# Storing the output of a residual matmul two tiles at a time, with semaphores of its own

## The chip, the core and the metric

The kernel runs on one NeuronCore of one Trainium2 chip. The metric is the device time of one execution in microseconds (us), the median of several runs. A profiled execution leaves a trace of every instruction and of every DMA packet. Engines are named as in the profile: PE (TensorE, the matmuls), PEld (its weight loads), DVE (VectorE), ACT (ScalarE), POOL (GpSimd) and SP (SyncE). ACT and SP issue DMAs here, each to a queue of its own; the transfers of both queues run on the same 16 DMA engines. "ACTq" and "SPq" in the profile are the issues of the two queues.

## What is computed

For each of 128 batch entries b, one of 8 weight matrices is picked by an index, and the product is added to the input:

```python
x = ...                      # (B=128, C=128, T=1024) float32
subjects = ...               # (128,) int32, 0..7
weights = ...                # (8, C=128, D=128) float32
w = weights[subjects]
out = x + jnp.einsum('bct,bcd->bdt', x, w)
```

Input and output are 67.1 MB each, the weights 0.5 MB, all in float32.

## The kernel before

**Tiles and slots.** A tile is four batch entries (G = 2 entries in each of H = 2 halves), 2.10 MB, and there are NT = 32 of them. SBUF holds SLOTS = 12 tiles in one tensor, x_all; tile i lives in slot i % 12. A tile's input is loaded into its slot, the sum is written over it in place, and the output is stored from there. So a slot is free for the load of tile i + 12 only when the store of tile i has landed.

**Loads.** ACT issues four loads of 512 KB for each tile (lines 203 to 207), in the order of the tiles. From tile 12 on it first waits until the slot's store has landed (line 205). Since ACT issues in order, a wait holds back every load behind it. POOL turns a landed tile into "ready" counts for PE (lines 209 to 214).

**Compute.** For each half of a tile, DVE copies the picked weights into a small tile (`place`), PE runs 8 matmuls into PSUM (`multiply`) and DVE adds the PSUM result to the slot (`add`), which raises s_added by one. So s_added counts two for each finished tile. PE starts on a tile when its four loads have landed.

**Stores.** SP issues the stores (lines 216 to 220). Tiles 0 to 19 are stored one by one; from tile 20 on two neighbours go in one store of 4.19 MB. A store of n tiles from tile i waits until s_added shows i + n + BEHIND finished tiles, with BEHIND = 4, and without BEHIND from tile 24 on (LAST = 8). A single store 0 thus waits for 5 finished tiles, store 1 for 6. The pair 20 waits for 26, the pair 22 for 28, the pair 24 (behind 22 in SP's order) for 26, the pair 26 for 28, and 28 for 30. The last pair, 30, is issued outside the loop (line 240) when all 32 are finished.

**Semaphores.** A slot has one semaphore, s_slot, for its loads and its store: each landed load and each landed store adds 16 to it. `emptied(i)` (line 123) computes the count at which the slot is free for tile i. In the last part each pair's store raises the even slot's semaphore alone. At the end ACT waits for the stores of the last 12 tiles.

**Queue order.** No order is worked out by a scheduler around the change: loads, readiness and stores stand in the program as the loops write them, on ACT, POOL and SP.

Of the kernel before, what the change touches and what calls it, by code (L numbers as in the profile page):

```python
# [30 lines left out]
G = 2  # L31
H = 2
# [3 lines left out]
SLOTS = 12  # L36

P_SLOTS = 2

BEHIND = 4  # L40
LAST = 8

PAIR = 2

DMA = 16

# [8 lines left out]
def transfer(nc, engine, out, in_):  # L55

    later, nc._always_lower_symbolic_ap = nc._always_lower_symbolic_ap, False
    ins, outs = engine.lower_ap_dma(in_), engine.lower_ap_dma(out)  # L60
    nc._always_lower_symbolic_ap = later
    return engine.add_instruction(
        mybir.InstDMACopy(
            name=nc.get_next_instruction_name(),
            engine=engine.engine,
            ins=ins,
            outs=outs,
            mode="Copy",
            cce_op=ALU.bypass,
            queue=QUEUES[engine.engine],  # L70
        )
    )


@with_exitstack
def kernel(
    ctx: ExitStack,
    tc: tile.TileContext,
    x: bass.AP,
    subjects: bass.AP,  # L80
    weights: bass.AP,
    out: bass.AP,
):
    nc = tc.nc
    B, C, T = x.shape
    S, _, D = weights.shape
    NT = B // (G * H)

    def sbuf(name, *shape, dtype=F32):
        return ctx.enter_context(nc.sbuf_tensor(name, list(shape), dtype)).ap()  # L90


    room = -(nc.sbuf_base + -nc.sbuf_base % 32) % ALIGN
    if room:
        sbuf("room", C, room // 4)
    x_all = sbuf("x_all", C, SLOTS * H * G * T)
    xs = [
        x_all[:, i * H * G * T : (i + 1) * H * G * T].rearrange("c (q t) -> c q t", t=T)
        for i in range(SLOTS)
    ]  # L100
    w_all = sbuf("w_all", C, S, D)
    ws = [sbuf(f"w{i}", C, 1, D) for i in range(H * G)]
    zeros = sbuf("zeros", C, N)
    given, near, wrap = (sbuf(name, 1, B, dtype=I32) for name in ("given", "near", "wrap"))
    index = sbuf("index", 1, B + H * G, dtype=I32)
    ps = [
        ctx.enter_context(nc.psum_tensor(f"ps{i}", [D, G, T], F32)).ap() for i in range(P_SLOTS)
    ]

    s_given = tc.alloc_semaphore("s_given")  # L110
    s_wall = tc.alloc_semaphore("s_wall")
    s_index = tc.alloc_semaphore("s_index")
    s_zeros = tc.alloc_semaphore("s_zeros")
    s_product = tc.alloc_semaphore("s_product")
    s_added = tc.alloc_semaphore("s_added")

    s_ready = tc.alloc_semaphore("s_ready")
    s_go = tc.alloc_semaphore("s_go")

    s_slot = [tc.alloc_semaphore(f"s_slot{k}") for k in range(SLOTS)]  # L120
    s_head = tc.alloc_semaphore("s_head")

    def emptied(i):
        turns = i // SLOTS
        return DMA * (H * G + 1) * turns - (DMA * G if i >= SLOTS and i % SLOTS == 0 else 0)

    def load(engine, i, q):
        transfer(
            nc,
            engine,  # L130
            xs[i % SLOTS][:, q, :],
            x[i * H * G + q].rearrange("(a r) t -> a (r t)", r=ROWS),
        ).then_inc(s_head if i * H * G + q < G else s_slot[i % SLOTS], DMA)

    def store(i, n):
        at = i % SLOTS * H * G * T
        return transfer(
            nc,
            nc.sync,
            out[i * H * G : (i + n) * H * G].rearrange("g d t -> d g t"),  # L140
            x_all[:, at : at + n * H * G * T].rearrange("d (o t) -> d o t", o=n),
        )

    def subjects_of(i):
        _, subject = nc.values_load_multi_w_load_instructions(
            index[0:1, i] if isinstance(i, slice) else index[0:1, bass.ds(i * (H * G), H * G)],
            engines=[mybir.EngineType.DVE],
            min_val=0,
            max_val=S - 1,
            skip_runtime_bounds_check_because="the index is clamped on the chip above",  # L150
        )
        return subject

    def place(h, subject):
        for q in range(h * G, (h + 1) * G):
            copy = nc.vector.tensor_copy(ws[q], w_all[:, bass.ds(subject[q], 1), :])  # L156
        copy.then_inc(s_go, 1)

    def multiply(slot, h):
        nc.tensor.wait_ge(s_go, 1).then_inc(s_go, -1)  # L160
        nc.tensor.wait_ge(s_ready, 1).then_inc(s_ready, -1)  # L161
        for q in range(h * G, (h + 1) * G):
            for t in range(0, T, N):
                at = slot * (H * G * T) + (q * T + t)
                mm = nc.tensor.matmul(  # L165
                    ps[h][:, q % G, t : t + N],
                    ws[q][:, 0, :],
                    x_all[:, bass.ds(at, N)],
                    start=True,
                    stop=True,  # L170
                )
        mm.then_inc(s_product, 1)

    def add(slot, h):
        mine = x_all[:, bass.ds(slot * (H * G * T) + h * G * T, G * T)]
        nc.vector.wait_ge(s_product, 1).then_inc(s_product, -1)  # L176
        nc.vector.tensor_tensor(  # L177
            mine, ps[h].rearrange("d g t -> d (g t)"), mine, ALU.add
        ).then_inc(s_added, 1)

    with tc.tile_critical():  # L181

        nc.sync.dma_start(given, subjects.rearrange("(o b) -> o b", o=1)).then_inc(s_given, DMA)
        nc.sync.dma_start(w_all, weights.rearrange("s c d -> c s d")).then_inc(s_wall, DMA)

        nc.vector.memset(zeros, 0.0).then_inc(s_zeros, 1)  # L186
        nc.tensor.wait_ge(s_zeros, 1)
        for _ in range(IDLE):
            nc.tensor.matmul(  # L189
                ps[P_SLOTS - 1][:, G - 1, :N], zeros[:, :D], zeros, start=True, stop=True  # L190
            )

        nc.vector.memset(index[:, B:], 0).then_inc(s_index, 1)  # L196
        nc.vector.wait_ge(s_given, DMA)
        nc.vector.tensor_scalar(near, given, -S, S - 1, ALU.max, ALU.min).then_inc(s_index, 1)  # L198
        nc.vector.wait_ge(s_index, 2)
        nc.vector.tensor_scalar(wrap, near, 0, S, ALU.is_lt, ALU.mult).then_inc(s_index, 1)  # L200
        nc.vector.wait_ge(s_index, 3)
        nc.vector.tensor_tensor(index[:, :B], near, wrap, ALU.add).then_inc(s_index, 1)  # L202
        for i in range(NT):
            if i >= SLOTS:
                nc.scalar.wait_ge(s_slot[i % SLOTS], emptied(i))
            for q in range(H * G):
                load(nc.scalar, i, q)

        for i in range(NT):
            if i == 0:  # L210
                nc.gpsimd.wait_ge(s_head, DMA * G).then_inc(s_ready, 1)
                nc.gpsimd.wait_ge(s_slot[0], DMA * G).then_inc(s_ready, 1)
            else:
                nc.gpsimd.wait_ge(s_slot[i % SLOTS], emptied(i) + DMA * H * G).then_inc(s_ready, H)

        for i in [*range(NT - SLOTS), *range(NT - SLOTS, NT, PAIR)]:
            n = 1 if i < NT - SLOTS else PAIR
            nc.sync.wait_ge(s_added, (i + n + (BEHIND if i < NT - LAST else 0)) * H)
            if i + n < NT:
                store(i, n).then_inc(s_slot[i % SLOTS], DMA)  # L220


        nc.vector.wait_ge(s_index, 4)
        nc.vector.wait_ge(s_wall, DMA)
        subject = subjects_of(slice(0, H * G))
        for h in range(H):
            place(h, subject)
        with nc.vector.Fori(0, NT) as turn:  # L228
            subject = subjects_of(turn + 1)
            for h in range(H):  # L230
                add(turn % SLOTS, h)
                place(h, subject)
        with nc.tensor.Fori(0, NT) as turn:
            for h in range(H):
                multiply(turn % SLOTS, h)

    with tc.tile_critical() as waits:
        for i in range(NT - SLOTS, NT - PAIR, PAIR):
            nc.scalar.wait_ge(s_slot[i % SLOTS], emptied(i + SLOTS))
    last = store(NT - PAIR, PAIR)  # L240

    tc.add_manual_dep(
        last.ins,
        waits.name,
        mybir.DependencyInfo(mybir.DependencyClass.NoSync, mybir.DependencyReason.SCHED_ONLY),
        reason="the end of the program waits for it",
    )
# [27 lines left out]
```

## Time and profile before

| What | Value |
|---|---|
| Runs of the kernel | 323.47 us median of 3 (323.29 to 323.54) |
| The profiled execution | 323.24 us |
| Its span in the trace | 321.5 us |
| HBM read and written | 67.63 MB and 67.11 MB, 419 GB/s over the span |
| PE busy | 249.8 us (78%) |
| DVE busy | 165.7 us (52%) |
| Mean granted PE clock | 0.905 |
| Loads of x | 128 of 512 KB, median 34.9 us from issue to landing |
| Single stores | 20 of 2048 KB, median 15.6 us from issue to landing |
| Paired stores | 6 of 4096 KB, median 28.6 us from issue to landing |
| Matmuls | 512, mean 635 ns |
| Adds | 64, mean 2291 ns |

The page shows the span in 40 slices of 8.04 us. Its row "DMA" gives the mean busy share of the 16 DMA engines in each slice as a digit of tenths, and the row "GB/s" what they moved. In the part on DMA queues, q10 carries the loads of x (ACT's queue) and q1 the stores, the weights and the index (SP's queue); the columns are packets, MB, and the time of the packets as a share of 16 engines' span.

The trace can also be asked for single transfers. Such an answer has two lines that matter: the issues (line, queue, operation, tensors, number; the shortest, middle and longest issue in ns; first and last start in us from the start of the span), and below it the shortest, middle and longest time from an issue to the landing of its data. A timeline line gives start, length, engine, line, operation and tensors, and in brackets the idle time of the engine before it.

### The profile page before, as it was taken

Reading aid. Unit: us, or ns where it says so; the run is one execution under the profiler, and the core shown is the slowest. Engines: PE = TensorE matmul, PEld = TensorE weight load, DVE = VectorE, ACT = ScalarE, POOL = GpSimd, SP = SyncE. Lnnn points to the kernel's source line nnn. Section 1 sums busy time; section 2 is a strip of 40 time slices with the busy share of each in tenths; the row PEclk is TensorE's granted clock in tenths of the full one; section 3 lists DMA queues with packets and bytes.
Section 4 is the critical chain, followed back from the end, with each engine's and each line's share of the span. In section 5 each row is a group of like instructions: output and inputs, shape, how many; then the busy total and the mean of one; then the engine's idle time right before and its main releaser. Section 6 shows DMA issues by size and latency. Waiting matters only on the chain. (4 is left out here: it accounts for less than half of the span.)

```text
span 321.5 us, 2368 instructions
## 1 busy us (share of the span) xinstructions
PE 249.8 (78%) x518; PEld 102.8 (32%) x518; DVE 165.7 (52%) x202; POOL 0.2 (0%) x4
## 2 busy tenths in 40 slices
PE   6999999999979666866888469999769995885000
PEld 2444444444433322322333124433323332331000
DVE  2377667767773366146365361776445766066000
POOL 0000000000000000000000000000000000000000
PEclk9999999999997799779999896999978999599555
DMA  7999999999999999999999999999999999999997
GB/s 283 428 424 424 426 424 391 428 426 426 428 432 428 423 430 424 426 424 424 426 426 428 430 430 426 426 426 428 424 424 424 420 426 430 426 428 424 430 424 318
DMA packets 11700, 134.76 MB, mean 419 GB/s; under 512 B 2482, under 2 KB 3507, under 8 KB 3507
## 3 DMA queue, kind: packets, MB, share of 16 engines
q10 hardware_dynamic: 6144, 67.12, 49.7%
q1 hardware_dynamic: 5554, 67.64, 49.7%
q14 instruction: 2, 0.01, 0.0%
HBM read 67.63 MB, written 67.11 MB: 419 GB/s over the span
## 5 line engine op out<-in xcount | busy, mean ns | idle before, releaser
L165 PE MATMUL ps<-x_all,w 128*128 x512 | 244.4, 635 | 42.2 <-PEq L161 27.6
L177 DVE TENSOR_TENSOR x_all<-ps,x_all 128x2048 f32 x64 | 146.6, 2291 | 124.9 <-DVEq L176 124.9
L165 PEld LDWEIGHTS ps<-x_all,w 128*128 128x128 f32 x512 | 101.0, 203 | 186.3 <-issue 185.8
L156 DVE COPY w<-w_all 128x128 f32 x132 | 23.1, 218 | 4.1 <-DMA w_all<-in_L_cond_weights_dram 4.1
L189 PE MATMUL ps<-zeros 128*128 128x512 f32 x6 | 5.5, 1088 | 1.7 <-DVE zeros L186 1.7
L189 PEld LDWEIGHTS ps<-zeros 128*128 128x128 f32 x6 | 1.8, 328 | 3.7 <-issue 2.1
L186 DVE MEMSET zeros<- 128x512 f32 x1 | 0.5, 485 | 1.0 <-SPq L181 1.0
L198 DVE TENSOR_SCALAR near<-given 1x128 int32<-1x128 int32 x1 | 0.2, 214 | 0.7 <-DMA given<-in_itok_B_dram 0.7
L202 DVE CUSTOM_DVE_ANT_0 index<-near,wrap 1x256 uint16<-1x256 uint16 x1 | 0.3, 280 | 0.0
L200 DVE TENSOR_SCALAR wrap<-near 1x128 int32<-1x128 int32 x1 | 0.2, 216 | 0.0
L262 POOL MEMSET const-bfloat16-1.0<- 128x1 bf16 x1 | 0.1, 101 | 0.0
L262 POOL MEMSET const-uint8-127<- 128x1 uint8 x1 | 0.1, 101 | 0.0
L262 POOL MEMSET const-float32-0.0<- 128x1 f32 x1 | 0.1, 98 | 0.2 <-issue 0.2
L262 POOL MEMSET const-float32-1.0<- 128x1 f32 x1 | 0.1, 98 | 0.0
L262 DVE BASE_LOAD x1 | 0.0, 21 | 0.1
L196 DVE MEMSET index<- 1x4 int32 x1 | 0.1, 62 | 0.0
## 6 DMA issues: line engine op xcount, KB each, us to landing
x_all<-in_x_dram ACTq DMA_DIRECT2D x128, 512.0 KB, 34.9
out_dram<-x_all SPq DMA_DIRECT2D x20, 2048.0 KB, 15.6
out_dram<-x_all SPq DMA_DIRECT2D x6, 4096.0 KB, 28.6
w_all<-in_L_cond_weights_dram SPq DMA_DIRECT2D x1, 512.0 KB, 5.0
given<-in_itok_B_dram SPq DMA_DIRECT2D x1, 0.5 KB
```

Of the source, the lines that this page charges most:

```text
L156: copy = nc.vector.tensor_copy(ws[q], w_all[:, bass.ds(subject[q], 1), :])
L165: mm = nc.tensor.matmul(ps[h][:, q % G, t : t + N], ws[q][:, 0, :], x_all[:, bass.ds(at, N)], start=True, stop=True,)
L177: nc.vector.tensor_tensor(mine, ps[h].rearrange("d g t -> d (g t)"), mine, ALU.add).then_inc(s_added, 1)
L186: nc.vector.memset(zeros, 0.0).then_inc(s_zeros, 1)
L189: nc.tensor.matmul(ps[P_SLOTS - 1][:, G - 1, :N], zeros[:, :D], zeros, start=True, stop=True)
L196: nc.vector.memset(index[:, B:], 0).then_inc(s_index, 1)
L198: nc.vector.tensor_scalar(near, given, -S, S - 1, ALU.max, ALU.min).then_inc(s_index, 1)
L200: nc.vector.tensor_scalar(wrap, near, 0, S, ALU.is_lt, ALU.mult).then_inc(s_index, 1)
L202: nc.vector.tensor_tensor(index[:, :B], near, wrap, ALU.add).then_inc(s_index, 1)
L262: nc = _bacc.Bacc("TRN2", target_bir_lowering=False, num_devices=1)
```

## The change

All stores become pairs. Each pair of slots has a semaphore for its store, s_store, and s_slot counts loads alone. SP's loop runs over even tiles and waits for i + 2 + BEHIND finished tiles with BEHIND = 3 (LAST stays 8), so that the pair 0 waits for 5, the pair 2 for 7, up to 25 for the pair 20 and 27 for 22; 24, 26 and 28 wait for 26, 28 and 30 as before. ACT waits before every second tile for the landing of the pair that used its two slots, and then issues eight loads. The number of stores goes from 26 to 16, ACT's waits in the load loop from 20 to 10. Tiles, loads, matmuls, adds and the last pair's place are as they were.

```diff
-BEHIND = 4
+PAIR = 2
+
+BEHIND = 3
 LAST = 8
-
-PAIR = 2
...
-    def emptied(i):
-        turns = i // SLOTS
-        return DMA * (H * G + 1) * turns - (DMA * G if i >= SLOTS and i % SLOTS == 0 else 0)
+    s_store = [tc.alloc_semaphore(f"s_store{k}") for k in range(SLOTS // PAIR)]
+
+    def stored(i):
+        return s_store[i % SLOTS // PAIR], DMA * (i // SLOTS + 1)
+
+    def loaded(i):
+        return s_slot[i % SLOTS], DMA * H * G * (i // SLOTS + 1) - (DMA * G if i % SLOTS == 0 else 0)
...
-    def store(i, n):
+    def store(i):
         at = i % SLOTS * H * G * T
         return transfer(
             nc,
             nc.sync,
-            out[i * H * G : (i + n) * H * G].rearrange("g d t -> d g t"),
-            x_all[:, at : at + n * H * G * T].rearrange("d (o t) -> d o t", o=n),
+            out[i * H * G : (i + PAIR) * H * G].rearrange("g d t -> d g t"),
+            x_all[:, at : at + PAIR * H * G * T].rearrange("d (o t) -> d o t", o=PAIR),
         )
...
         for i in range(NT):
-            if i >= SLOTS:
-                nc.scalar.wait_ge(s_slot[i % SLOTS], emptied(i))
+            if i >= SLOTS and i % PAIR == 0:
+                nc.scalar.wait_ge(*stored(i - SLOTS))
             for q in range(H * G):
                 load(nc.scalar, i, q)
...
-                nc.gpsimd.wait_ge(s_slot[0], DMA * G).then_inc(s_ready, 1)
+                nc.gpsimd.wait_ge(*loaded(0)).then_inc(s_ready, 1)
             else:
-                nc.gpsimd.wait_ge(s_slot[i % SLOTS], emptied(i) + DMA * H * G).then_inc(s_ready, H)
-
-        for i in [*range(NT - SLOTS), *range(NT - SLOTS, NT, PAIR)]:
-            n = 1 if i < NT - SLOTS else PAIR
-            nc.sync.wait_ge(s_added, (i + n + (BEHIND if i < NT - LAST else 0)) * H)
-            if i + n < NT:
-                store(i, n).then_inc(s_slot[i % SLOTS], DMA)
+                nc.gpsimd.wait_ge(*loaded(i)).then_inc(s_ready, H)
+
+        for i in range(0, NT, PAIR):
+            nc.sync.wait_ge(s_added, (i + PAIR + (BEHIND if i < NT - LAST else 0)) * H)
+            if i + PAIR < NT:
+                store(i).then_inc(stored(i)[0], DMA)
...
         for i in range(NT - SLOTS, NT - PAIR, PAIR):
-            nc.scalar.wait_ge(s_slot[i % SLOTS], emptied(i + SLOTS))
-    last = store(NT - PAIR, PAIR)
+            nc.scalar.wait_ge(*stored(i))
+    last = store(NT - PAIR)
```

## The prediction

> **What bounds the kernel now.** First I read the DMA rows of the page.
>
> ```profile
> DMA  7999999999999999999999999999999999999997
> GB/s 283 428 424 424 426 424 391 428 426 426 428 432 428 423 430 424 426 424 424 426 426 428 430 430 426 426 426 428 424 424 424 420 426 430 426 428 424 430 424 318
> q10 hardware_dynamic: 6144, 67.12, 49.7%
> q1 hardware_dynamic: 5554, 67.64, 49.7%
> ```
>
> From the second slice to the last but one the 16 engines never rest: loads alone (slices 2 to 5), both together, and stores alone (the last four whole slices) all move about 427 GB/s. The two queues share 99.4% of the span. A tile of 2.10 MB therefore costs 2.097 / 0.427 = 4.91 us of DMA, and the time is the sum of the bytes. No edit can make it much shorter; it gets longer if both queues are ever empty together. So I look for that place. While loads run there is none: the middle load takes 34.9 us from issue to landing, and 4.91/0.4 = 12 us of that would be one tile, so about three tiles stand queued. The end is another matter. Queue waits of SP, then the last tile's loads, matmuls, adds and store:
>
> ```profile
> SPq L271 <- DMA out_dram<-x_all: 23.1, 1, 23.1
> ...
> L62 ACTq DMA_DIRECT2D x_all<-in_x_dram x2: 2260/2576/2891, 240.8 to 243.1; - x2
> DMA to landing us min/median/max: 42.2/42.6/43.0
> ...
> 274.85 10.14 PE L165 MATMUL ps<-x_all,w 128*128 x16 [5.21 <-PEq L161]
> 286.53 7.13 PE L165 MATMUL ps<-x_all,w 128*128 x16 [1.54 <-PEq L161]
> 293.90 2.29 DVE L177 TENSOR_TENSOR x_all<-ps,x_all 128x2048 f32 x1 [0.81 <-DVEq L176]
> ...
> L62 SPq DMA_DIRECT2D out_dram<-x_all x1: 601/601/601, 296.8 to 296.8; - x1
> DMA to landing us min/median/max: 23.7/23.7/23.7
> ```
>
> The last load lands at 243.1 + 43.0 = 286.1, the last add ends at 293.90 + 2.29 = 296.2, the last store is issued 0.6 later and lands at 320.5. It holds 4.19 MB, 9.8 us of DMA, so of its 23.7 us some 9 to 10 were spent behind older stores. **Those 9 us are the slack**: the last add may come that much later for nothing, and after that each us is a us of the run.
>
> **The rates that decide the end.** Four stores, two single and two paired, and two pairs of loads:
>
> ```profile
> L62 SPq DMA_DIRECT2D out_dram<-x_all x1: 663/663/663, 46.4 to 46.4; - x1
> DMA to landing us min/median/max: 13.6/13.6/13.6
> ...
> L62 SPq DMA_DIRECT2D out_dram<-x_all x1: 544/544/544, 53.5 to 53.5; - x1
> DMA to landing us min/median/max: 15.1/15.1/15.1
> ...
> L62 SPq DMA_DIRECT2D out_dram<-x_all x1: 612/612/612, 237.1 to 237.1; - x1
> DMA to landing us min/median/max: 21.9/21.9/21.9
> ...
> L62 SPq DMA_DIRECT2D out_dram<-x_all x1: 607/607/607, 257.0 to 257.0; - x1
> DMA to landing us min/median/max: 21.5/21.5/21.5
> ```
>
> ```profile
> L62 ACTq DMA_DIRECT2D x_all<-in_x_dram x2: 882/970/1059, 207.5 to 208.6; - x2
> DMA to landing us min/median/max: 34.9/35.9/36.9
> ...
> L62 ACTq DMA_DIRECT2D x_all<-in_x_dram x2: 2281/2584/2888, 214.4 to 217.3; - x2
> DMA to landing us min/median/max: 37.2/37.3/37.3
> ```
>
> The singles land at 60.0 and 68.6: 8.6 us a tile while loads run beside them, a share of 4.91/8.6 = 0.57. The first had an empty queue, so 13.6 - 8.6 = 5.0 us of it is start and finish. The page's last slice holds 8.04 x 318/427 = 6.0 us of traffic, which ends at 319.4 against the landing at 320.5; so 1.1 us is the finish and 3.9 the start. The pairs then drain in 16.9 and 16.5 us, mean 16.7: a share of 9.82/16.7 = 0.588. The loads beside the first pair land at 245.5 and 254.6, three loads on: 12.1 us a tile, share 0.40, which would give the pair 0.60. I take 0.588 (a whole pair, with its edges), so a load tile beside pairs takes 4.91/0.412 = 11.9 us, and keep 0.57 and 0.605 as ends. From a tile's landing to its last add I count 10.0 us for the last tile (286.1 to 296.2) and 13.0 for the one before (last load issued at 237.6, 36.9 to landing, add done at 287.5), whose 16 matmuls took 10.14 us at a lower clock. I take 11.5, or 10 where TensorE had waited under 2 us.
>
> **The change part by part.** *Fewer, larger stores*: 26 become 16, on SP. Ten issues of 0.54 us go from a queue that waits most of the time: nothing. Ten times 16 semaphore writes go from the engines; the page counts 2482 packets under 512 B. Bounds: nothing, and the step from 427 to 428 GB/s that the slices allow between mixed traffic and large stores alone, 0.2% of the 230 us that change, 0.5 us. I take 0.1, nearer to nothing, since slices with loads of 512 KB alone move the same as those with 4 MB stores.
>
> The Trainium skill, page "SBUF — State Buffer", section "The DMA setup-cost knee", gives each DMA a fixed 2 us and advises the largest transfers; ten fewer would by that be worth 20 us (an estimate from the page). The slices disagree: 512 KB loads alone run at 424 to 428 GB/s, so the cost overlaps here.
>
> *One wait of ACT for two slots* (L205): the even slot's loads are issued one single store later, 8.6 us. Behind that wait only loads stand. They join a queue with some 35 us to landing, which hides it; were that queue empty, each would be late in full. *POOL's waits* keep their number and meaning: nothing. *Own semaphores*: no instruction more on the path.
>
> *BEHIND 3 on pairs* (L218): pair i waits for i+5 added tiles, as single i did; the odd tile goes one add earlier. The pairs 20 and 22 wait for 25 and 27 where they waited for 26 and 28, and 24 follows 22 at once. So the store queue is ahead, and the loads, which get only 0.41 beside it, come in later; the bytes are the same. Ledger, with pair, issue, data from and to:
> - 0 at 46.4, 50.3 to 67.8 (0.7 for the slow slice 7: 8.04 x 35/426); 2, 4, 6, 8 follow without a gap to 84.5, 101.2, 117.9, 134.6, as loads come every 11.9 us.
> - 10 at 133.5 (tile 14 landed at 122.0, plus 11.5), 137.4 to 154.1. Loads had 2.8 us alone, in which they go 2.4 times as fast.
> - 12 at 152.5, 156.4 to 173.1; 14 at 172.4, 176.3 to 193.0; 16 at 192.5, 196.4 to 213.1; 18 at 212.2, 216.1 to 232.8; 20 at 231.2, 235.1 to 251.8; 22 at 250.8, 254.7 to 271.4. Gaps of 2.3 to 3.4 us.
> - 24 to 288.1; tile 24 lands at 220.3, then 11.9 us each less what the gaps give, tile 31 at 296.3; 26 to 301.1, alone from 296; 28 to 310.9.
> - Last add 296.3 + 11.5 = 307.8; issue 308.4; data from 312.3.
>
> The engines are empty from 310.9 to 312.3: **1.4 us**. The same ledger for the kernel before, at the singles' share, ends its loads at 285.4 where the trace has 286.1. Sum on the profiled execution's 323.24 (span 321.5, 1.7 around it): 323.24 - 0.1 + 1.4 = 324.5. The runs' median lies 0.23 above that execution, so 324.7; I write 324.6.
>
> Ends: with the lag between 10 and 13 and the share between 0.57 and 0.605, the last add falls between 303 and 310, the hole between nothing and 3.9 us. It is near the edge because a later add shifts the gaps too.
>
> **Rivals.**
> - *The slack suffices* (no slower). The last add stays before about 306, because the gaps in the store queue fall long and let the loads through. For it: half of the ledgers within the ends; 7 of the 9 us of slack must be used up before anything shows. Against: the odd stores go earlier in every round. Time: 323.47 - 0.1, about 323.4.
> - *The larger store gains*. Each transfer costs something that the overlap does not hide; 0.5 us at most by the slices, with the slack left: 322.8. Against: loads alone show no such cost. The skill's knee, above, is the rule for this one.
> - *The store queue takes two thirds.* If an engine's turn grew with the store, 16 pieces against 8, loads would take 14.7 us a tile, and the ledger's last add comes at 310 to 315: a hole of 3 to 8 us, 329. Against: the pairs of the trace show 0.60 at most. The Trainium skill, "DMA: Bandwidth & Descriptors", section "Queues, rings and completion order", has each engine change queues after a whole packet; that no row shows what a packet is here leaves this open.
> - *The change is not what it says*: no; the program has 16 stores of 128x8x1024 and no single one.
>
> **How the numbers follow.** Hole of 0.7 to 4 us 0.48, slack suffices 0.42, larger store gains 0.05, two thirds 0.05. A measurement of this kernel can tell about 0.2%, 0.65 us, from no change. Faster 0.05, same 0.42, slower 0.53. The predicted time is the first case's, 324.6; its own range is 324.1 to 327.0. The range for all goes from 323.0, the slack case with its gain, to 327.0, the hole of 3.9 less the gain; the two-thirds case and the gain case are left out.
>
> **What would show it.** Right: the last load lands at 293 to 298 and the last store at 306 to 311, with some 14 us to landing instead of 23.7, and the GB/s row dips in its last two slices. If that store still takes 17 us or more, the slack held. Loads of a tile landing under 11.5 us apart, or long stretches without stores, would make the share wrong; a dip anywhere earlier would mean that I missed an empty queue.

## The result, and the profile after

The changed kernel takes 324.37 us (median of 16 runs, 323.32 to 326.12) against 323.35 us (16 runs, 322.98 to 323.87) of the kernel before: ratio 1.0035, 95% interval 1.002 to 1.005. It is slower by about 1.0 us. Three of its runs lie at 325.7 us or more and thirteen at 324.7 or less, so it also scatters over 2.8 us where the kernel before scatters over 0.9. The profiled execution is one of the three: 325.97 us, span 324.2.

The page of the changed kernel, rows on DMA:

```profile
DMA  7999999999999999999999999999999999999967
GB/s 281 427 423 427 435 423 396 425 423 431 427 431 425 424 427 429 423 425 421 431 427 421 429 423 427 431 421 427 427 427 427 427 425 431 427 425 429 427 287 323
...
q10 hardware_dynamic: 6144, 67.12, 49.4%
q1 hardware_dynamic: 5394, 67.63, 49.2%
```

The last slice but one moves 287 GB/s where it moved 424 before; (427 - 287)/427 x 8.1 us = 2.7 us of traffic are missing there. The end of this execution, by the loads of the last tile, the matmuls of the last two tiles, the last add and the last store:

```profile
L62 ACTq DMA_DIRECT2D x_all<-in_x_dram x3: 2276/2888/2908, 245.5 to 251.3; - x3
DMA to landing us min/median/max: 46.1/46.2/46.6
...
286.68 8.82 PE L169 MATMUL ps<-x_all,w 128*128 x16 [2.11 <-PEq L165]
298.33 10.16 PE L169 MATMUL ps<-x_all,w 128*128 x16 [2.83 <-DVE w L160]
...
308.74 2.29 DVE L181 TENSOR_TENSOR x_all<-ps,x_all 128x2048 f32 x1 [0.81 <-DVEq L180]
...
L62 SPq DMA_DIRECT2D out_dram<-x_all x1: 600/600/600, 311.6 to 311.6; - x1
DMA to landing us min/median/max: 11.6/11.6/11.6
...
310.00:313.00 3.00, 0.00 (x0) 0.00 (x0) 1.30 (x3) 0.00 (x0) 0.72 0.20 87
```

The last line is a stretch of the window view; its last three columns are the granted clock, the share of the DMA engines and GB/s. The last load lands at 297.9 (before: 286.1), the last tile's matmuls take 10.16 us at a lower clock (granted 0.50 from 298.3 to 304.5, against 7.13 us at 1.00 for the last tile before), the last add ends at 311.0, and the engines stand four fifths idle from 310 to 313. Such a stretch, in which both queues are empty, is called a hole below. The last store then lands 11.6 us after its issue: it found nothing ahead of it.

A second trace of the same kernel (323.94 us, span 322.2) looks different at the same place:

```profile
294.61 8.82 PE L169 MATMUL ps<-x_all,w 128*128 x16 [4.58 <-PEq L165]
...
303.68 2.29 DVE L181 TENSOR_TENSOR x_all<-ps,x_all 128x2048 f32 x1 [0.81 <-DVEq L180]
...
L62 SPq DMA_DIRECT2D out_dram<-x_all x1: 601/601/601, 306.6 to 306.6; - x1
DMA to landing us min/median/max: 14.6/14.6/14.6
...
310.00:313.00 3.00, 0.00 (x0) 0.00 (x0) 0.00 (x0) 0.00 (x0) 0.50 0.99 421
```

The last add ends at 306.0, 5 us earlier, and no engine rests: 0.99 busy, 421 GB/s. The store still stands some 3 us behind older ones (14.6 against 11.6). Yet its span is 0.7 us longer than the kernel before's. A third trace (324.01 us) has the same end. So a hole explains the one of the three longest runs that was traced, and something else is needed for the rest. The two later traces are of runs somewhat below the median of 324.37; a run at the median was not traced.

### The profile page after: what moved, and what is told of

It is laid out like the page before. It is cut to its first block, busy times and chain, and to the rows that moved or that the text cites. A ratio compares the mean times of both kernels' runs of the same rounds, so it can differ in the third digit from the quotient of the medians.

```text
span 324.2 us, 2358 instructions
## 1 busy us (share of the span) xinstructions
PE 258.4 (80%) x518; PEld 105.8 (33%) x518; DVE 165.7 (51%) x202; POOL 0.2 (0%) x4
## 5 line engine op out<-in xcount | busy, mean ns | idle before, releaser
L169 PE MATMUL ps<-x_all,w 128*128 x512 | 252.9, 653 | 48.5 <-PEq L165 45.6
L169 PEld LDWEIGHTS ps<-x_all,w 128*128 128x128 f32 x512 | 104.0, 209 | 198.1 <-issue 197.6
```

The source lines that it names most:

```text
L169: mm = nc.tensor.matmul(ps[h][:, q % G, t : t + N], ws[q][:, 0, :], x_all[:, bass.ds(at, N)], start=True, stop=True,)
```

## The experiments

Each kernel was timed beside the kernel before on the same chip, and each ratio is to that. Three chips were used: one for experiments 1 to 4, one for 5, 9, 10 and 11, one for 6, 7, 8 and 12; the kernel before took 323.30, 323.19 and 323.29 us on them. Theory T, or H, is the prediction's: the hole before the last pair. Theory R, later S, is that the 4 MB stores cost something of their own.

**1. Pairs held for one tile more** (`BEHIND = 3` becomes `4` in the changed kernel).

> The changed kernel with BEHIND = 4: pairs wait for one more tile. Theory T (each store goes out at an earlier tile count, so the loads end late and the last pair finds empty queues): last load lands at 285 to 292, last add at 296 to 304, no hole; 323.3 us, ratio to before 0.999 to 1.001. Rival P (pairing itself, by its larger share and by freeing two slots at once): the last load still lands after 294 and a hole of 1 us or more stays, ratio 1.002 to 1.005. Rival R (4 MB stores slow the engines all along): ratio 1.002 or more with the last store's landing over 17 us after its issue.

Measured: 324.32 us, ratio 1.0032 (1.0022 to 1.0042). The last load lands at 286.8 and the last store of its trace is:

```profile
L62 SPq DMA_DIRECT2D out_dram<-x_all x1: 602/602/602, 297.4 to 297.4; - x1
DMA to landing us min/median/max: 23.7/23.7/23.7
```

The loads end as early as before the change and the store has its old 23.7 us, so there is no hole. And the time is still that of the changed kernel. T is right on the loads and wrong on the time; what fits is R: a loss with no hole possible, since the last store still stood 12 us behind older ones (23.7 against the 11.6 of a store with nothing ahead).

**2. Singles released one tile earlier** (`BEHIND = 4` becomes `3` in the kernel before).

> The kernel before with BEHIND = 3: single stores as before, each one tile earlier; the pairs from tile 20 on wait as in the changed kernel. Theory T: last load lands at 290 to 297, last add at 301 to 308, the slack shrinks from 9 us to 0 to 6 us and in some runs is gone; ratio 1.000 to 1.003. Rival P: the last load lands before 289 and the last store still takes over 20 us to land; ratio 0.999 to 1.001.

Measured: 323.49 us, ratio 1.0003 (0.9994 to 1.0012). In its trace:

```profile
L62 SPq DMA_DIRECT2D out_dram<-x_all x1: 600/600/600, 303.1 to 303.1; - x1
DMA to landing us min/median/max: 17.5/17.5/17.5
```

The last store is issued 6.3 us later than in the kernel before. The earlier release alone eats most of the slack, as T said, without pairs, and while slack is left it costs nothing.

**3. The last pair stored as two singles.**

```diff
-        for i in range(0, NT, PAIR):
+        for i in range(0, NT - PAIR, PAIR):
...
+        nc.sync.wait_ge(s_added, (NT - 1) * H)
+        store(NT - PAIR, 1).then_inc(stored(NT - PAIR)[0], DMA)
+        nc.sync.wait_ge(s_added, NT * H)
...
-    last = store(NT - PAIR)
+    last = store(NT - 1, 1)
```

> The changed kernel with the last pair stored as two singles, the first as soon as tile 30 is finished. Theory T: nothing moves ahead of it; tile 30's store (4.9 us) fills the wait for tile 31, so a hole of up to 4 us goes; 323.3 us, ratio 0.999 to 1.001, the last store lands 7 us or more after its issue, and the last load still lands at 293 to 298. Rival R: ratio stays 1.002 to 1.005.

Measured: 324.05 us, ratio 1.0021 (1.0012 to 1.0031), highest run 325.04. Its trace has no hole, and its last add ends early, at 303.7, so that it would have had none with a pair either. None of the 11 runs reaches the 325.7 of the changed kernel's three longest, which with 11 runs can be chance. The greater part of the loss stays with the place of the hole filled: against T as the cause of the median.

**4. Pairs released two tiles earlier** (`BEHIND = 1`).

> The changed kernel with BEHIND = 1: pairs wait for two tiles fewer, the suspected cause doubled and more. Theory T: last load lands at 301 to 306, last add near 314, a hole of 4 to 10 us; 327 to 333 us, ratio 1.013 to 1.03. Rivals P and R: stores earlier than this cost nothing new, ratio 1.002 to 1.006.

Measured: 331.38 us, ratio 1.0237 (1.0218 to 1.0255). Window view of its end:

```profile
303.00:310.00 7.00, 7.00 (x18) 2.89 (x16) 5.12 (x6) 0.00 (x0) 1.00 1.00 424
310.00:318.00 8.00, 4.00 (x10) 1.51 (x8) 5.12 (x6) 0.00 (x0) 0.89 0.01 4
318.00:328.00 10.00, 0.00 (x0) 0.00 (x0) 0.00 (x0) 0.00 (x0) 0.50 0.98 419
```

While PE and DVE finish the last tile, all DMA engines rest for 8 us, as much as the whole loss (8.1 us). The last add ends at 316.5, later still than expected. The mechanism of the hole is shown; experiments 1 and 3 show that it is not what the median run pays.

**5. Two stores of 2 MB for each pair, waits unchanged.**

```diff
-        return s_store[i % SLOTS // PAIR], DMA * (i // SLOTS + 1)
+        return s_store[i % SLOTS // PAIR], DMA * PAIR * (i // SLOTS + 1)
...
-                store(i).then_inc(stored(i)[0], DMA)
+                for j in range(i, i + PAIR):
+                    store(j, 1).then_inc(stored(i)[0], DMA)
```

> The changed kernel, waits and tile counts as they are, but each pair but the last is stored by two DMAs of 2 MB issued one behind the other, on the pair's semaphore. Theory H (the median's 1 us is the hole before the last pair): the loads end as late as in the changed kernel, ratio 1.002 to 1.004. Theory S (the 4 MB store itself slows some of the 16 engines, hole or not): ratio 0.999 to 1.001 where there is no hole.

Measured: 323.50 us, ratio 1.0003 (0.9993 to 1.0014). Two DMAs of 2 MB in place of one of 4 MB take away nearly all of the loss. But this trace's last load lands at 287.9, not as late as H assumed, so the hole went as well, and this run alone does not decide. Experiment 6 has no hole on either side.

**6. The same with BEHIND = 4**, to be set beside experiment 1.

> The kernel with pairs and BEHIND = 4, each pair but the last stored by two DMAs of 2 MB: no hole with either size of store. Theory S (one 4 MB store makes some of the 16 engines late): ratio 0.999 to 1.001, against 1.0032 with the 4 MB stores; the last part of the last store lands 0.4 to 0.6 us after the mean of its 16 parts. Rival U (two slots freed at once, or the semaphores): ratio 1.002 to 1.004, the last part 0.9 us or more behind the mean.

Measured: 323.30 us, ratio 1.0001 (0.9990 to 1.0011), against 1.0032 (1.0022 to 1.0042) with 4 MB stores. The last store of its trace:

```profile
L62 SPq DMA_DIRECT2D out_dram<-x_all x1: 612/612/612, 298.8 to 298.8; - x1
DMA to landing us min/median/max: 22.0/22.0/22.0
```

The intervals are apart, the waits, the slots and the number of semaphores are the same, and neither trace has a hole (22.0 and 23.7 us to landing): **storing each pair in one DMA of 4 MB, and not in two of 2 MB, costs about 1 us**. The expectation on the parts of the last store failed, though: its last part lands 1.05 us behind the mean of the 16, not 0.4 to 0.6.

**7 and 8. Where the 4 MB stores cost.** In the changed kernel, 4 MB stores for tiles 0 to 11 alone, or for the pairs after tile 12 alone; the other pairs but the last are two stores of 2 MB. The core of the second (the first has the opposite condition):

```diff
+    def pieces(i):
+        return PAIR if i < SLOTS else 1
...
+                for j in range(i, i + PAIR, PAIR // pieces(i)):
+                    store(j, PAIR // pieces(i)).then_inc(stored(i)[0], DMA)
```

> The changed kernel with 4 MB stores for tiles 0 to 11 alone, where the next store is always queued behind; the later pairs but the last are two DMAs of 2 MB each. Theory S1 (an engine falls behind where a 4 MB store ends with no other queued): as two_singles, ratio 0.999 to 1.001. Theory S2 (every 4 MB store makes engines late): ratio 1.001 to 1.002.

> The changed kernel with two DMAs of 2 MB for each pair of tiles 0 to 11 and one store of 4 MB for each later pair, most of which end with no other queued. Theory S1: as the changed kernel, ratio 1.002 to 1.004, the last part of the last store 0.9 us or more behind the mean of the 16 unless a hole came before it. Theory S2: ratio 1.001 to 1.002.

Measured: first 323.50 us, ratio 1.0007 (0.9998 to 1.0016); after 323.87 us, ratio 1.0023 (1.0013 to 1.0032). The cost is seen with the later stores, as S1 said, but this does not show S1. The two intervals overlap a little, and the later stores are 9 of the 15 pairs that were varied: the loss of 1.0035 shared equally among the 15 would give 1.0014 and 1.0021, inside both intervals.

**9. Pairs held for two tiles more** (`BEHIND = 5`).

> The changed kernel with BEHIND = 5, one more step away from any hole: last load at 278 to 286, last store 20 us or more to landing. Theory H: ratio 0.999 to 1.001. Theory S: ratio 1.002 to 1.004, as with BEHIND = 4.

Measured: 327.10 us, ratio 1.0124 (1.0106 to 1.0143). Neither theory had this. The GB/s row of its page, and two stretches:

```profile
GB/s 275 432 420 426 430 424 432 420 422 246 426 424 426 434 426 421 426 424 434 424 422 428 430 428 424 424 424 436 424 422 424 424 430 430 424 424 424 436 428 307
```

```profile
66.00:73.00 7.00, 7.00 (x17) 2.91 (x16) 5.07 (x7) 0.00 (x0) 1.00 0.97 414
73.00:77.00 4.00, 4.00 (x11) 1.84 (x10) 2.87 (x4) 0.00 (x0) 1.00 0.50 107
```

The hole is at the front. The first pair now goes out when 7 tiles are finished (60.6 us) and lands at 74; the twelve slots' loads are all in by 64, and nothing may be loaded or stored until the pair has landed. So for pairs the count of tiles has a hole on either side: BEHIND = 5 starves the start, 1 the end.

**10. Every store single.**

```diff
-        for i in [*range(NT - SLOTS), *range(NT - SLOTS, NT, PAIR)]:
-            n = 1 if i < NT - SLOTS else PAIR
+        for i in range(NT):
+            n = 1
...
-    last = store(NT - PAIR, PAIR)
+    last = store(NT - 1, 1)
```

> The kernel before with every store single, the last twelve tiles and the last one too (BEHIND = 4 and LAST = 8 as before). Theory H: no change, ratio 0.999 to 1.001. Theory S: the six pairs at the end cost something too; ratio 0.997 to 0.9995.

Measured: 323.20 us, ratio 0.9999 (0.9991 to 1.0008). The six pairs that the kernel before has at its end cost nothing that can be seen. Had each cost as much as a fifteenth of the changed kernel's loss, the ratio would be 0.9986, below the interval; so the place of a 4 MB store matters. No version tried beats the kernel before.

**11 and 12. The changed kernel again**, for its trace.

> The changed kernel as it is, for a second trace; its runs lie between 323.3 and 326.1 us. Theory H: a run of 324.0 to 324.8 us has both queues empty for 0.7 to 1.5 us before its last store. Theory S: such a run has no hole or one under 0.4 us, the last store takes 12 us or more to landing, and the landings of its 16 parts lie 1.3 us or more apart where the kernel before has 0.9.

> The changed kernel a third time, for its trace. Theory S: if it takes 323.3 to 324.8 us, no hole, and the mean landing of the last store's parts is within 0.4 us of the 320.1 of the kernel before, with the last part 0.7 us or more behind it; if it takes 325.5 us or more, a hole of 1.5 us or more and parts within 0.3 us of each other.

Measured: 323.94 and 324.01 us, no hole in either. What the traces' DMA records say of the 16 engines, in us (landing of the 16 parts of the last store; "slow" is the time beyond 615.8 ns of all 16 KB packets over 640 ns after the first 60 us, summed over 16 engines):

```
kernel                        mean landing   last part   behind the mean   slow
before                           320.10        320.50         0.40          3.2
all singles                      320.10        320.64         0.54          0.4
singles, BEHIND 3                319.88        320.62         0.74          0.2
two singles                      319.76        321.02         1.26          0.8
two singles, BEHIND 4            319.75        320.80         1.05          2.5
4 MB for the first 12            319.97        320.61         0.64          1.2
4 MB after the first 12          319.87        320.94         1.07          3.4
last pair split                  320.16        321.28         1.12          6.4
changed, second trace            320.06        321.18         1.12          7.1
changed, third trace             320.37        321.24         0.87          7.7
changed, BEHIND 4                320.33        321.08         0.75         12.4
```

The run ends when the latest engine ends: each traced time is that of the last part plus 2.7 to 2.8 us. In the four lower rows, with 4 MB stores throughout and no hole, the last part lands at 321.1 to 321.3, 0.6 to 0.8 us after the kernel before's.

One part of this is slow packets. The four rows have 6.4 to 12.4 us of them, 0.4 to 0.8 us for each engine, against 0.2 us and less in the others. Beside the two singles with the same waits, the mean landing is 0.3 to 0.6 us later (320.06 and 320.37 against 319.76; 320.33 against 319.75). Beside the kernel before it is at most 0.3 us later, since the first 60 us, which the column leaves out, have 16.8 us of slow packets there and 9.3 to 16.2 in the four rows, for reasons that no run here separates. Counted over the whole span, a sixteenth of the slow packets plus 318.9 us gives the mean landing of all eleven traces within 0.15 us.

After 60 us most of the slow packets come in clusters of about 1 us, some 2 to 3.5 us before the landing of a 4 MB store when no data of a next store follow yet (in the second trace at 171, 212 and 249 us, with landings at 174.3, 214.8 and 251.2). Not every such store has one. The kernel before has one as well, at the end of its pair 20 (2.9 of its 3.2 us).

The other part is that some engines end later than others, and that is not peculiar to 4 MB stores: the two rows of two singles have it too, in single traces that lie 0.3 us above their kernels' medians. The traces thus account for only some of the 1 us that the medians show: the runs traced with 4 MB stores lie up to 0.5 us below their medians, and for experiments 1 and 6 the traced runs differ by 0.28 us where the medians differ by 1.0. Why a 4 MB store ends so, and what makes one engine late, stays open.

## Why the prediction was right or wrong

**Time and direction were right**: 324.6 us forecast, 324.37 measured, within the range, slower with the larger chance. **That the sum comes so close is in part luck**: the 1.4 us that it adds for a hole are not what the median run pays, and the larger store, which it has as a gain of 0.1, costs about 1 us.

- *The loads come in later and eat the slack*: right. Forecast 293 to 298 for the last load, 297.9 and about 294 traced; last store 306 to 311, traced 311.6 and 306.6. The paired store's drain of 16.7 us was right: the first four pairs land 17.0, 16.7 and 16.8 us apart. Experiment 2 shows the earlier release eating slack by itself.
- *A hole of 1.4 us*: right in kind, wrong as the median's price. The profiled execution has 2.7 us, the two others none. Two sizes were off and partly balanced. The start of the last store was taken as 3.9 us, from stores beside loads, plus 0.6 of issue; with empty queues issue to landing is 11.6 us for 9.8 us of data, 1.8 us for start and finish together where 5.0 was counted. So the slack was 23.7 - 11.6 = 12.1 us, not 9, and the last harmless add is at 296.2 + 12.1 = 308.3, not 306. Against it, the last tile ran at the low clock in the profiled execution, 13 us from landing to add, the upper end of what was bounded. For the same reason the sign "some 14 us to landing" was misread: 14.6 is what the two traces without a hole show, the one with a hole has 11.6.
- *Fewer, larger stores: a gain of 0.1 us, bounded by 0 and 0.5*: the step that failed, and its sign was not in the bounds. "Slices with loads of 512 KB alone move the same as those with 4 MB stores" was read from rows that round to 1 GB/s, 0.23%, which is 0.7 us of the span: the size of the thing looked for. It was also read at the end of the kernel before, where the 4 MB stores cost nothing (experiment 10), and the first of its four slices of "stores alone" still has loads up to 286.1. The 4 MB store costs about 1 us (1.0032 against 1.0001). The rival by which larger transfers gain is refuted with it (its 322.8 should read 323.0, 0.5 off 323.47). The fixed cost of each DMA that the Trainium skill states ("SBUF — State Buffer", "The DMA setup-cost knee") does not decide here, where the transfers overlap: fewer DMAs took longer.
- *ACT's wait for two slots is hidden*: right at BEHIND 3. The two singles keep that wait and cost nothing. Its cover is not large, though: at BEHIND 5 no load is left in the queue when the first pair lands, and the run loses 3.9 us.
- *Semaphores of their own*: nothing, as said; the two singles have them too.

## What to carry to other kernels

When the DMA engines are busy for the whole span, look for the first and the last moment at which both queues can be empty together; the count that holds a store back moves both. Of the counts tried for pairs here, 1 had a hole at the end, 3 one in some runs and 5 one at the start; only the trace with 4 has none. Larger transfers need not gain when transfers already overlap, and here they lost 0.3%: compare the sizes with the same waits, by time and not by a rounded rate. One profiled run can show a cost that the median run does not pay; take a second trace when the runs scatter more than before.

## What was not expected of the hardware

- A store issued while loads are queued needs about 5.0 us beyond its own traffic (13.6 us for a single whose neighbours land 8.6 apart); one issued to empty queues needs 1.8 us (11.6 us for 4 MB, in the profiled execution and at `BEHIND = 1`).
- A hole puts the 16 engines in step again: after it the parts of the last store land within 0.2 us of each other (323.03 to 323.19 in the profiled execution, 0.16 us at `BEHIND = 1` too), where the eleven traces without one have 0.9 to 1.8 us.
